# A message-passing layer: six edge chunks of unequal size, three packed lists, and eight quads whose rows are gathered from x and multiplied on the chip

## The chip, the core and the metric

The kernel runs on one core of a Trainium2 chip. The metric is the time of one execution on the device in microseconds; lower is better. The kernel before took 831.66 us (median of three runs, 831.54 to 835.16). A core has five engines, each of which runs its own instructions in program order: TensorE (PE in the profile, PEld its weight loads), VectorE (DVE), ScalarE (ACT), GpSimd (POOL) and SyncE (SP), which here only issues DMAs. Engines wait for each other through semaphores. SBUF is the memory on the chip, PSUM holds TensorE's sums, and DRAM tensors lie outside.

## What is computed

The input is a graph of 12,500 nodes with 128 features each (`x`) and 400,000 edges, sorted by their destination `dst`. Each edge has a source `src` and a length `d`.

```python
rbf = exp(-(d[:, None] - centers) ** 2 / (2.0 * width * width))      # 50 centers from 0 to 10
cut = 0.5 * (cos(pi * d / 10) + 1.0) * (d <= 10)
W = (silu(rbf @ fw1 + fb1) @ fw2 + fb2) * cut[:, None]
messages = (x[src] @ pw + pb) * W
agg = segment_sum(messages, dst)
y = x + (silu(agg @ mw1 + mb1) @ mw2 + mb2)
out = layernorm(x + y)
```

An edge longer than 10 counts for nothing, since `cut` is zero there. With these inputs 71,145 of the 400,000 edges remain.

## The kernel before, in words

**Order of the work.** The program order of every engine is written out by hand (`manual_schedule`). Python generators and loops decide it while the kernel is built; on the chip it is fixed, and an engine that waits holds all that stands behind in its order.

**Packing.** The edges come in five chunks of 128 rows of 625 edges. For each chunk `pack(c)`, a generator, drops the edges that are too long. VectorE counts how many are gone before each one (`gone`, `step`), joins step, destination and source in one word (`nodes`), and moves the words and the lengths to the left in ten passes by powers of two (lines 340 to 361). A row of at most 160 survivors (`CAP`, the tile `line`) is then written by one GpSimd scatter (line 382) to its place in the DRAM tensor `packed`. Rows overlap with zeros at their ends, so even rows go to one list and odd rows to another (`side`). The lists are cleared first. A read-back (`pair`, line 393) takes both lists and ORs them. The unpacking then gives source indices (`srci`), local destinations (`dl`), cutoff factors (`cut`) and bases, each turned by TensorE and copied to its place, and stores the lengths to DRAM (`near_d`). `yield` values are estimates of VectorE's time; the callers spend them as a budget (`advance`). Chunk 0 is read back by GpSimd, the others by SyncE.

**Projection.** Meanwhile all of `x` is loaded in 25 tiles of 512 nodes, turned (`turn`), multiplied by `pw` with the bias `pb` (`project`) and stored to the DRAM tensor `proj`. A bias is used as a sum of three bf16 parts, which VectorE makes (`in_parts`).

**The loop over quads.** A quad is 512 packed edges; there are 141. `fetch(q)` gathers the quad's rows of `proj` by four indirect DMAs from GpSimd (line 490) into one of eight buffers `got`. `radial`, `basis`, `first`, `tanh`, `silu` and `second` compute W for it. `message` multiplies (line 560), which frees the buffer. `place` makes one-hot matrices from `dl` and `cut` (line 568), `sum_up` multiplies with them, and `add` adds the sums into `aggT` (line 595), a 128 x 12,500 tile in SBUF that GpSimd has cleared. In each turn of the loop quad q + 3 is fetched (`AHEAD`), and VectorE goes on with packing the next chunks (`QB` tells which quads a chunk serves).

**Nodes.** From quad 70 on (`NODES`), whenever the sums of 512 nodes are final, the node network and the layer norm run between the quads; the rest follows after the last quad. Behind everything stands a branch that computes the whole again without packing; with these inputs it is not taken.

Of the kernel before, what the change touches and what calls it, by code (L numbers as in the profile page):

```python
# [29 lines left out]
RB = 8  # L30
CAP = 160


QB = (0, 26, 54, 81, 109, 141)
NC_ = len(QB) - 1
NQ = QB[-1]
AHEAD = 3
GOT = 8

# [6 lines left out]
def kernel(  # L46
# [40 lines left out]
    R = E // (NC_ * P)  # L87
# [3 lines left out]
    assert H == P and E == NC_ * P * R and E % P == 0 and W <= N <= 1 << SB  # L91
    assert CAP <= R < 1 << (32 - RB - SB) and 2 * MW % P == 0
# [32 lines left out]
    def load_rows(c):  # L125

        raw[c] = []
        for name, ap, dt in (("r_d", edge_weight, I32), ("r_dst", dst, I32), ("r_src", src, I32)):
            t = work.tile([P, R], dt, name=name, bufs=2)
            v = ap[c * P * R:(c + 1) * P * R].rearrange("(r l) -> r l", r=P)  # L130
            nc.sync.dma_start(t, v if ap is not edge_weight else v.bitcast(I32))
            raw[c].append(t)
# [9 lines left out]
    zero_i = keep.tile([P, 2 * MW // (4 * P)], I32, name="zero_i")  # L142
    nc.gpsimd.memset(zero_i, 0)
    packed = dram.tile([2, MW], I32, name="packed")
    for k in range(4):
        nc.gpsimd.dma_start(packed.rearrange("s (k w) -> (s k) w", k=P // 2)
                            .rearrange("p (q w) -> p q w", q=4)[:, k], zero_i)
    aggT = keep.tile([P, N], F32, name="aggT")

    def clear(a, b):  # L150

        for n0 in range(a, b, 500):
            nc.gpsimd.memset(aggT[:, n0:min(n0 + 500, b)], 0.0)

    clear(0, 3500)
# [18 lines left out]

    def load_weights():
        for p0 in (0, 64):
            nc.sync.dma_start(w1_sb[p0:p0 + NUM_RBF], fw1)
            nc.sync.dma_start(w1_sb[p0 + NUM_RBF:p0 + KR], row(fb1))
        return (load_bias("fb2", fb2), load_bias("mb1", mb1), load_bias("mb2", mb2),
                load("fw2_sb", [H, H], fw2), load("mw1_sb", [H, H], mw1),  # L180
                load("mw2_sb", [H, H], mw2))
# [12 lines left out]
    for name in ("pb", "fb2", "mb1", "mb2"):  # L194
# [9 lines left out]
    nc.vector.tensor_scalar(before, iota_n[:, :P], part_f, None, op0=OP.is_gt)  # L204

    side_i = keep.tile([P, 1], I32, name="side_i")
    nc.vector.tensor_scalar(side_i, part_i, 1, None, op0=OP.bitwise_and)
    side = keep.tile([P, 1], F32, name="side")
    nc.vector.tensor_scalar(side, side_i, float(MW), None, op0=OP.mult)

    end = keep.tile([P, 1], F32, name="end")
    nc.vector.tensor_scalar(end, part_f, 2.0, float(2 * NQ * QE), op0=OP.mult, op1=OP.add)

    k_f = keep.tile([P, 1], F32, name="k_f")
    nc.vector.tensor_scalar(k_f, part_f, 64.0, -64.0, op0=OP.is_ge, op1=OP.mult)
    nc.vector.tensor_add(k_f, k_f, part_f)
    rbf_scale = keep.tile([P, 1], F32, name="rbf_scale")
    nc.vector.tensor_scalar(rbf_scale, k_f, float(NUM_RBF), None, op0=OP.is_lt)  # L220
    rbf_bias = keep.tile([P, 1], F32, name="rbf_bias")
    nc.vector.tensor_scalar(rbf_bias, k_f, -CUTOFF / (NUM_RBF - 1), rbf_scale,
                            op0=OP.mult, op1=OP.mult)

    def in_parts(name, t):
        b = bias_b[name]
        p = keep.tile([96, H], BF16, name=name + "_p")
        for k in range(3):
            nc.vector.tensor_copy(p, t)
            nc.vector.tensor_copy(b[32 * k:32 * k + 1],  # L230
                                  p[32 * k:32 * k + 1, None, :].to_broadcast([1, 4, H]))
            if k < 2:
                nc.vector.tensor_sub(t, t, p)
        return b
# [22 lines left out]
    for c in range(NC_):  # L257
        nc.vector.tensor_scalar(lim[:, c:c + 1], part_f[:64], float(2 * QB[c] - DONE[1]), 0.0,
                                op0=OP.add, op1=OP.max)
    nc.vector.scalar_tensor_tensor(lim, lim, DONE[0], lim, op0=OP.mult, op1=OP.mult)  # L260
# [26 lines left out]
    bits = (R - 1).bit_length()  # L287
    LB = RB + SB

    def rowed(dt, name, n=R, bufs=1):  # L290
        return work.tile([P, n], dt, name=name, bufs=bufs)

    def pack(c):

        if c + 1 < NC_:
            load_rows(c + 1)
        r_d, r_dst, r_src = raw[c]
# [5 lines left out]
        yield 0.6  # L303
        gone = rowed(F32, "gone")
        nc.vector.tensor_tensor_scan(gone, drop, drop, 0.0, op0=OP.add, op1=OP.max)
        yield 1.4
# [4 lines left out]
        yield 0.9  # L311
# [10 lines left out]
        yield 0.6  # L322
        relc = rowed(F32, "drop")
        nc.vector.tensor_scalar(relc, rel, -127.5, None, op0=OP.add)
        yield 0.4
        nc.vector.tensor_reduce(span[:, c:c + 1], relc, AX.X, OP.max, apply_absolute_value=True)
        yield 0.7
# [4 lines left out]
        yield 0.3  # L332
# [3 lines left out]
        yield 0.7  # L336
        nc.vector.scalar_tensor_tensor(nodes, step, LB, nodes, op0=OP.logical_shift_left,
                                       op1=OP.bitwise_or)
        yield 0.7
        for b in range(bits):  # L340
# [6 lines left out]
            yield 0.4  # L347
            m = go[:, k:n + k]
            if b < bits - 1:
# [4 lines left out]
                yield 0.7  # L354
# [4 lines left out]
            yield 0.7  # L359
            nc.vector.copy_predicated(r_d[:, :n], m, r_d[:, k:n + k])  # L360
            yield 0.7
# [15 lines left out]
        line = work.tile([P, CAP, 2], I32, name="line", bufs=2)  # L377
# [3 lines left out]
        yield 0.6  # L381
        nc.gpsimd.indirect_dma_start(
            out=packed.rearrange("s (w o) -> (s w) o", o=1),
            out_offset=bass.IndirectOffsetOnAxis(ap=at_i[:, 0:1], axis=0),
            in_=line.rearrange("p e w -> p (e w)"), in_offset=None)
        if c == 0:
            clear(3500, N)
        yield -3
# [3 lines left out]
        pair = work.tile([64, 2, 512], I32, name="pair", bufs=1)  # L392
# [67 lines left out]

    xT_of = {}

    def turn(t0):
        r = rows(t0)
        n = sum(r)
        xp = bank("pu")
# [323 lines left out]
    for k, t0 in enumerate(tiles):  # L790
        if k + 6 < len(tiles):
            load_x(tiles[k + 6])
        if k == 4:
            weights = load_weights()
# [166 lines left out]
```

## Time and profile before

| what | value |
|---|---|
| median of the runs | 831.66 us |
| profiled execution | 830.76 us |
| its span, first to last instruction | 829.0 us |
| instructions | 11346 |
| TensorE, share of the span busy | 71% |
| VectorE | 82% |
| GpSimd | 70% |
| ScalarE | 31% |
| bytes moved by DMA | 90.62 MB |
| first gather of rows starts | 71.60 us |
| first message starts | 85.73 us |
| last gather starts | 801.92 us |

A line of a group reads: source line, engine, operation, tile written <- tiles read, how many, then busy time in us and the mean of one in ns, and after the second bar the idle time of the engine just before them and what ended it. "issue" is time in which an engine waited for nothing that the profile shows. A line of a timeline reads: start and length in us, then the instruction, and in brackets the engine's idle time before it and what ended that. The granted clock is TensorE's, as a share of full speed.

### The profile page before, as it was taken

How to read it: one execution, taken by the hardware profiler on the slowest of the kernel's cores; microseconds unless marked ns; L12 is line 12 of the kernel's file. 1: busy time of each engine (PE TensorE's matmuls, PEld its weight loads, DVE VectorE, ACT ScalarE, POOL GpSimd, SP SyncE). 2: the span in 40 equal slices, each digit the busy share in tenths (PEclk: the TensorE clock that was granted, in tenths of full speed). 3: DMA queues.
4: the chain of work that ended last, by engine and by line, in shares of the span. 5: the costliest groups of instructions: out<-in, count | busy, mean ns of one | idle time of the engine just before them, and what ended most of it. 6: DMA issues, size and time to landing. Idle time of an engine off the chain costs nothing.

```text
span 829.0 us, 11346 instructions
## 1 busy us (share of the span) xinstructions
PE 588.0 (71%) x3356; PEld 449.8 (54%) x3356; DVE 679.6 (82%) x1822; ACT 257.6 (31%) x397; POOL 578.6 (70%) x613
## 2 busy tenths in 40 slices
PE   4792766666667766776767687787877876867862
PEld 4680545455555555555555465555655664646651
DVE  7967899989999998999968888777867667667774
ACT  2454322132222322232222233523434424521521
POOL 3045777777777777777777777777777777777750
PEclk9995788878887788768896799998999988999887
DMA  8994324232153323233333442722623623632421
GB/s 245 265 309 122 96 64 128 72 103 76 49 151 77 90 73 80 58 97 88 88 83 92 102 118 77 195 66 78 181 77 89 169 80 87 171 99 52 122 61 41
DMA packets 85700, 90.62 MB, mean 109 GB/s; under 512 B 13623, under 2 KB 64851, under 8 KB 85632
## 3 DMA queue, kind: packets, MB, share of 16 engines
q1 hardware_dynamic: 66464, 49.95, 21.1%
q0 software_dynamic: 18912, 39.77, 19.4%
q8 instruction: 28, 0.46, 0.2%
q14 instruction: 40, 0.33, 0.1%
q10 hardware_dynamic: 256, 0.11, 0.1%
HBM read 74.71 MB, written 15.07 MB: 108 GB/s over the span
## 4 chain that ended last, share of the span: by engine, by line
DVE 33%; POOL 17%; PE 16%; DMA 15%; issue 14%; DVEq 3%; ACT 1%; SPq 1%; POOLq 0%; ACTq 0%
POOL got L490 16%; DMA got<-proj,srci 11%; DVE hot L568 8%; DVE s L542 4%; PE pa L577 4%; DVE msg L560 3%; DVE aggT L595 3%; PE ph L529 3%; PE pu L554 3%; DMA x<-in_x_dram 3%; DVEq L585 2%; DVE r_d L360 2%; PE pa L242 1%; PE ms L242 1%; DVE st L629 1%
## 5 line engine op out<-in xcount | busy, mean ns | idle before, releaser
L490 POOL DMA_INDIRECT got<-proj,srci x564 | 553.8, 982 | 171.9 <-issue 146.6
L577 PE MATMUL pa<-hot,msg 128*128 128x128 f32 x1128 | 184.6, 315 | 107.1 <-DVE msg L560 106.8
L577 PEld LDWEIGHTS pa<-hot,msg 128*128 128x128 f32 x1128 | 164.3, 224 | 121.4 <-DVE msg L560 121.3
L554 PEld LDWEIGHTS pu<-fw_h,s 128*128 128x128 f32 x1128 | 176.2, 223 | 12.0 <-issue 5.1
L554 PE MATMUL pu<-fw_h,s 128*128 128x128 f32 x1128 | 174.8, 306 | 0.0
L568 DVE TENSOR_SCALAR hot<-iota_n,dl,cut 128x128 f32<-128x128 f32 x564 | 158.0, 356 | 0.8 <-PE pa L577 0.6
L535 ACT ACTIVATE t<-ph 128x1024 f32<-128x1024 f32 (+1 forms) x71 | 71.8, 1012 | 268.5 <-PE ph L529 255.0
L529 PE MATMUL ph<-rbf,w_sb 51*128 51x512 f32 x282 | 101.3, 791 | 63.9 <-DVE s L542 53.3
L560 DVE TENSOR_TENSOR msg<-pu,got 128x512 f32<-128x512 f32 x141 | 96.3, 683 | 60.4 <-DMA got<-proj,srci 49.1
L542 DVE SCALAR_TENSOR_TENSOR s<-t,ph 128x1024 f32<-128x1024 f32 (+1 forms) x71 | 85.7, 1207 | 6.8 <-ACT t L535 6.7
L595 DVE TENSOR_TENSOR aggT<-aggT,pa 128x128 f32 x282 | 79.9, 283 | 7.5 <-PE ms L607 2.3
L529 PEld LDWEIGHTS ph<-rbf,w_sb 51*128 51x128 f32 x282 | 27.8, 224 | 85.3 <-issue 52.6
L551 PE MATMUL pu<-fb_b,ones_b 96*128 96x512 bf16 x141 | 61.7, 438 | 0.0
L609 ACT ACTIVATE zt<-ms 128x512 f32<-128x512 f32 (+1 forms) x25 | 14.6, 587 | 150.3 <-PE ms L607 150.3
L519 ACT ACTIVATE rbf<-d,rbf_bias,rbf_scale 128x512 f32<-128x512 f32 (+1 forms) x71 | 57.1, 804 | 0.2
L668 ACT ACTIVATE x<-x,by,rs 128x128 f32<-128x128 f32 x91 | 37.3, 482 | 59.4 <-DVE by L638 59.4
L551 PEld LDWEIGHTS <-ones_b 96*128 96x128 bf16 x141 | 14.9, 105 | 73.7 <-issue 73.2
L520 ACT ACTIVATE rbf<-rbf 128x512 f32<-128x512 f32 (+1 forms) x71 | 44.7, 630 | 2.2
L351 DVE SCALAR_TENSOR_TENSOR nodes<-go,nodes 128x625 int32<-128x625 int32 x45 | 36.5, 810 | 1.3
L360 DVE COPY_PREDICATED r_d<-go,r_d 128x624 int32<-128x624 int32 (+9 forms) x50 | 36.9, 739 | 0.0
L355 DVE COPY_PREDICATED nodes<-go,nodes 128x624 int32<-128x624 int32 (+8 forms) x45 | 35.9, 798 | 1.2
L626 DVE SCALAR_TENSOR_TENSOR x<-x,ms 128x512 f32<-128x512 f32 x23 | 15.8, 686 | 24.9 <-PE ms L242 24.9
(159 smaller groups left out, 501.1 us busy)
## 6 DMA issues: line engine op xcount, KB each, us to landing
d<-near_d SPq DMA_DIRECT2D x137, 128.0 KB
x<-in_x_dram SPq DMA_DIRECT2D x48, 256.0 KB
got<-proj,srci POOLq DMA_INDIRECT x564
proj<-hp SPq DMA_DIRECT2D x24, 256.0 KB
out_dram<-x SPq DMA_DIRECT2D x24, 256.0 KB
r_d<-in_edge_weight_dram SPq DMA_DIRECT2D x5, 312.5 KB
r_dst<-in_dst_dram SPq DMA_DIRECT2D x5, 312.5 KB
r_src<-in_src_dram SPq DMA_DIRECT2D x5, 312.5 KB
```

The lines of the kernel that those rows point to most:

```text
L360: nc.vector.copy_predicated(r_d[:, :n], m, r_d[:, k:n + k])
L490: nc.gpsimd.indirect_dma_start(out=got[:, j, :], out_offset=None, in_=proj, in_offset=bass.IndirectOffsetOnAxis(ap=i, axis=0))
L519: nc.scalar.activation(rbf[:u], d[:u], AF.Square, bias=rbf_bias[:u], scale=rbf_scale[:u])
L529: nc.tensor.matmul(ph[:, h, :], w1_sb[p0:p0 + KR], rbf[p0:p0 + KR], start=True, stop=True)
L535: nc.scalar.activation(t[:, :n], ph[:, :n], AF.Tanh, scale=0.5)
L542: nc.vector.scalar_tensor_tensor(s[:, :n], t_of.pop(o)[:, :n], 1.0, ph[:, :n], op0=OP.add, op1=OP.mult)
L551: nc.tensor.matmul(pu, ones_b[:, :P], bias_b["fb2"].rearrange("k j f -> k (j f)"), start=True, stop=False)
L554: nc.tensor.matmul(pu[:, j * H:(j + 1) * H], s[:, j * P:(j + 1) * P], fw2_h, start=False, stop=(j == QT - 1))
L560: nc.vector.tensor_mul(msg, pu_of.pop(q).rearrange("p (j f) -> p j f", j=QT), got_of.pop(q))
L568: nc.vector.tensor_scalar(hot[:, j, :], iota_n[:, :W], dl[:, at[0], at[1]], cut[:, at[0], at[1]], op0=OP.is_equal, op1=OP.mult)
L577: nc.tensor.matmul(pa[:, k * W:(k + 1) * W], msg[:, j, :], hot[:, j, :], start=(j % 2 == 0), stop=(j % 2 == 1))
L595: nc.vector.tensor_add(to, to, pa[:, k * W:(k + 1) * W])
```

## The change

- **Chunks.** Six chunks of 180, 435, 600, 640, 640 and 630 edges a row (`ROWS`, `CAPS`, `QB`). The number of passes follows from the width: eight, nine and ten.
- **Three lists.** A row goes to the list of its number modulo 3; the read-back takes three lists and needs one more OR. The lists are cleared in three stages (`clear_packed`), the first by GpSimd, the others by SyncE (at tile 12 and behind quad 1).
- **Rows of x.** The first eight quads (`FROM_X`) are gathered from `x` instead of `proj`, before the projection is finished, and turned and multiplied by `pw` in their buffers (`multiply`).
- **Clearing.** ScalarE clears `aggT` by copies scaled by zero (`clear`): ten pieces of 500 during the projection, the other fifteen from quad 32 on. Bases of chunks 0 to 2 stay below 5000.
- **Parts of a bias.** ScalarE makes the bf16 copies (`part_of`); VectorE keeps the subtraction.
- **Order by estimated times.** Estimates of VectorE's time now depend on the width (`one`, `two_a_cycle`). A clock of VectorE (`clock`), one of GpSimd (`pool`) and the times at which rows have landed (`there_at`) decide where a fetch, a packing step, a multiplication or a read-back is put into the orders (`fetches`, `multiplies`, `pack_until`). Fetches may now stand up to eight quads ahead (`GOT`) instead of three. The read-backs' lengths (`radials`) are copied by SyncE alone; two of these four pairs were GpSimd's in the kernel before.

```diff
-CAP = 160
-QB = (0, 26, 54, 81, 109, 141)
+ROWS = (180, 435, 600, 640, 640, 630)
+CAPS = (58, 128, 160, 166, 166, 164)
+QB = (0, 7, 26, 52, 80, 109, 141)
...
+FROM_X = 8
 GOT = 8
+CLEARED = 5000
+CLEAR_Q = 32
+CLEAR_C = 2
+PACK_US = (1.4, 1.0)
...
-    packed = dram.tile([2, MW], I32, name="packed")
-    for k in range(4):
-        nc.gpsimd.dma_start(packed.rearrange("s (k w) -> (s k) w", k=P // 2)
-                            .rearrange("p (q w) -> p q w", q=4)[:, k], zero_i)
+    packed = dram.tile([3, MW], I32, name="packed")
+    def clear_packed(k, eng):
+        a, b = CLEAR[k:k + 2]
+        for i in range(3):
+            v = packed[i, a:b].rearrange("(p w) -> p w", p=P)
+            for w0 in range(0, (b - a) // P, 376):
+                n = min(376, (b - a) // P - w0)
+                eng.dma_start(v[:, w0:w0 + n], zero_i[:, :n])
+    clear_packed(0, nc.gpsimd)
...
-        for n0 in range(a, b, 500):
-            nc.gpsimd.memset(aggT[:, n0:min(n0 + 500, b)], 0.0)
+    def clear(pieces=1, to=N):
+        while pieces and to_clear and to_clear[0][0] < to:
+            a, b = to_clear.pop(0)
+            nc.scalar.activation(aggT[:, a:b], iota_n[:, :b - a], AF.Copy, scale=0.0)
+            pieces -= 1
...
+    def part_of(name, t, k):
+        p = keep.tile([96, H], BF16, name=f"{name}_p{k}")
+        nc.scalar.copy(p, t)
+        nc.scalar.copy(bias_b[name][32 * k:32 * k + 1],
+                       p[32 * k:32 * k + 1, None, :].to_broadcast([1, 4, H]))
+        if k < 2:
+            nc.vector.tensor_sub(t, t, p)
...
+    def one(n):
+        return 0.1 + 0.00115 * n
+    def two_a_cycle(n):
+        return 0.1 + 0.0007 * n
...
+    def fetches(until, most):
+        while fetched[0] < min(most, known[0]) and pool[0] <= until:
+            q = fetched[0]
+            fetch(q, table=x if q < FROM_X else None)
+            pool[0] = max(pool[0], summed.get(q - GOT, 0.0)) + 5.15
+            there_at[q] = pool[0] + 2.2
+            fetched[0] += 1
...
+        fetches(clock[0], most[0])
+        pool[0] = max(pool[0], clock[0]) + 1.35
         nc.gpsimd.indirect_dma_start(
             out=packed.rearrange("s (w o) -> (s w) o", o=1),
...
+        awake[c] = pool[0] + (2.6 if c == 0 else 3.5)
...
+        nc.vector.tensor_tensor(pair[:np_, 0], pair[:np_, 0], pair[:np_, 1], OP.bitwise_or)
+        yield 0.6
+        nc.vector.tensor_tensor(length, pair[:np_, 0, 1::2], pair[:np_, 2, 1::2], OP.bitwise_or)
...
+    def multiply(q):
+        turn("got", got_of[q])
+        h = bank("pa").rearrange("p (k f) -> p k f", k=4)
+        rows_times(h, xT_of.pop("got"), pw_sb, bias_b["pb"], [P] * 4)
+        nc.scalar.copy(got_of[q], h)
...
+    def pack_until(us, ahead=2):
+        while clock[0] < us and todo:
+            c = next((c for c in todo[:ahead] if awake[c] <= clock[0]), None)
+            if c is None:
+                clock[0] = min([us] + [awake[c] for c in todo[:ahead]])
+            else:
+                go_on(c)
+    def multiplies(until):
+        while times[0] < min(FROM_X, fetched[0]) and there_at[times[0]] <= until:
+            multiply(times[0])
+            times[0] += 1
...
     for k, t0 in enumerate(tiles):
...
+        if loads and k >= 4:
+            nc.sync.dma_start(*loads.pop(0))
+        if k == 12:
+            clear_packed(1, nc.sync)
+        if k == 18:
+            load_rows(2)
+        if k in (19, 20, 21):
+            part_of("fb2", fb2_f, k - 19)
         project(t0)
+        clear(1, CLEARED)
...
+        upto = 12.0 + 2.1 * k
+        fetches(upto, FROM_X)
+        multiplies(upto)
+        pack_until(upto, 1 if 0 in todo and 1 not in todo else 2)
+        if k >= 16:
+            radials(3)
...
     for q in range(NQ):
         nodes(q)
-        if q + AHEAD < NQ:
-            fetch(q + AHEAD)
+        most[0] = min(NQ, q + GOT)
+        fetches(clock[0], most[0])
+        fetches(math.inf, min(NQ, q + AHEAD + 1))
+        multiplies(max(clock[0], there_at[min(q + 1, NQ - 1)]))
+        if q >= CLEAR_Q:
+            clear()
+        radials(q // 2 + 5)
...
-        left = 1.3 if q % 2 == 0 else 2.5
-        for c in list(todo[:2]):
-            if rest[c]:
-                rest[c] -= 1
-            elif left > 0:
-                left = advance(c, left)
+        clock[0] = max(clock[0], there_at[q])
+        summed[q] = clock[0] + 0.7
+        clock[0] += 2.2 if q % 2 else 3.4
+        if q == 1:
+            clear_packed(2, nc.sync)
+        if q + 1 < NQ:
+            pack_until(max(there_at[q + 1], clock[0] + PACK_US[min(todo, default=0) > CLEAR_C]))
```

## The prediction

> **What bounds the kernel now.** I read the page's busy shares first, then the chain, then GpSimd's own waits and its timeline, and last VectorE in two stretches. VectorE looks like the bound by share (82% against GpSimd's 70%), but shares hide idle time that an engine cannot avoid.
>
> From the page (part 1, the chain, the group of the gather):
>
> ```profile
> PE 588.0 (71%) x3356; PEld 449.8 (54%) x3356; DVE 679.6 (82%) x1822; ACT 257.6 (31%) x397; POOL 578.6 (70%) x613
> DVE 33%; POOL 17%; PE 16%; DMA 15%; issue 14%; DVEq 3%; ACT 1%; SPq 1%; POOLq 0%; ACTq 0%
> L490 POOL DMA_INDIRECT got<-proj,srci x564 | 553.8, 982 | 171.9 <-issue 146.6
> ```
>
> The 564 gathers (four for each of 141 quads) cost 982 ns each, and each has 171.9/564 = 0.305 us of idle time ahead of it, nearly all "issue": GpSimd waits for nobody. Its own list of waits (total, times, longest) says the same: no entry of a gather has a longest wait over 0.3 us, and the long ones lie ahead of the first gather.
>
> ```profile
> POOL got L490 <- issue: 146.6, 481, 0.3
> POOL packed L382 <- DVE first L300: 40.6, 1, 40.6
> POOL near_d L402 <- DVE length L401: 8.1, 1, 8.1
> POOL got L490 <- DMA got<-proj,srci: 7.9, 26, 0.3
> ```
>
> Its timeline gives the ends of that stretch (start, length, then the instruction):
>
> ```profile
> 48.95 1.06 POOL L382 DMA_INDIRECT packed<-line,at_i  x1 [40.59 <-DVE first L300]
> ...
> 71.60 1.18 POOL L490 DMA_INDIRECT got<-proj,srci  x1 [0.30 <-DVE part L277]
> ```
>
> and, further on, quad 8's first gather and the last gather of all:
>
> ```profile
> 113.33 1.31 POOL L490 DMA_INDIRECT got<-proj,srci  x1 [0.30 <-issue]
> ...
> 801.92 0.94 POOL L490 DMA_INDIRECT got<-proj,srci  x1 [0.30 <-issue]
> ```
>
> From 71.60 to 802.86 GpSimd goes from gather to gather: 564 x (0.982 + 0.305) = 725.9, plus four scatters of packed rows at about 1.35 with their gap, 731.3 in all. So the span is 71.6 before the first gather + 731.3 + 26.1 after the last (829.0 - 802.86). VectorE is a close second. In 85 to 425 us, while lists are packed between the quads, it is busy 318.87 of 340 us and its list of waits shows no wait for a gather from 100 to 400; afterwards it is busy 281.76 of 378.
>
> ```profile
> 85.00:425.00 340.00, 239.75 (x1273) 184.56 (x1271) 318.87 (x769) 85.17 (x107) 261.94 (x257) 0.80 0.32 86
> 425.00:803.00 378.00, 287.09 (x1679) 214.53 (x1680) 281.76 (x852) 130.24 (x216) 286.18 (x301) 0.90 0.41 107
> ```
>
> The columns are PE, PEld, DVE, ACT, POOL, clock, DMA share and GB/s.
>
> **The change, part by part.** What matters is when the gathers of quad 8 and later can run. Eight buffers hold gathered rows, so quad 8's gather waits until quad 0's message is made. From there on GpSimd has the same 133 quads to gather, 802.86 - 113.33 = 689.5 us, and the same 26.1 behind it. So I time quad 0's message.
>
> *Chunk 0 packed (180 edges a row in place of 625).* VectorE does this. A shifting pass of 625 took 3.0 us (four instructions: 0.50, 0.81, 0.86, 0.74 by the groups of L345, L351, L355, L360), and instructions of 113 to 160 columns took 0.23 to 0.33. Between these, a pass takes 1.15 at 180 columns and 2.3 at 435. The bias's casts move to ScalarE, where a 128x512 copy takes 0.59. The bias landed at 6.07 in before, so VectorE's first subtraction of it, which now stands ahead of the scan, holds the scan to about 6.6. Then come scan 0.5, the seven small side instructions 0.9 (0.13 each), counts, steps and the second subtraction 0.7, the offsets up to the first joined word 2.3, seven passes 7.6 (the last are narrower), the last pass 0.6 and seven line instructions 1.4: the scatter starts at 20.6, where it stood at 48.95. Scatter 1.1, landing 2.5 (the chain's landings of gathers are 2.3 to 2.8), read-back 0.7 to issue and 2.5 to land give 27.4. VectorE fills that wait with 1.7 us of small instructions, which had lain before the packing, and chunk 1's head. From the read-back to the indices took 66.36 to 68.56 = 2.2; the third list adds an OR of 512 words, about 0.65 (twice the 0.41 of 256 less the overhead). Indices at 30.3, **first gather at 30.5 instead of 71.6**. The four copies of lengths that GpSimd issued ahead of it (522 ns each) go to SyncE. The 25 clears of 532 ns leave GpSimd; only 18 of them (8.3 us) stood behind the first scatter, beside waiting for it, so they are inside the 41 us and not added again. On ScalarE 25 x 0.59 = 15 us lie in an engine that is busy 31%; ten are in the projection, the others at quads 32 to 46, each between two additions into the same sums. A clear finds its addition done a quad earlier, so I cost these at nothing; 15 x 0.6 = 9 us on VectorE if that cover is gone.
>
> *Gathers beside the packing.* Here one rule of the Trainium skill speaks against the change. The rows: from 100 to 400 us, beside packing, a gather took 1022 ns; from 500 to 800, with none, 947 ns.
>
> ```profile
> L490 POOL DMA_INDIRECT got<-proj,srci x224 | 228.9, 1022 | 68.3 <-issue 59.7 <-DMA got<-proj,srci 4.0 <-DVE aggT L595 2.4
> L490 POOL DMA_INDIRECT got<-proj,srci x240 | 227.2, 947 | 73.1 <-issue 59.7 <-DVE aggT L595 4.3 <-DMA got<-proj,srci 2.7
> ```
>
> The skill's page "SBUF — State Buffer", section "A bandwidth-pool intuition that's wrong (but worth ruling out)", says that GpSimd cannot write descriptors while VectorE holds the port they share: a GpSimd-issued DMA of some 620 ns alone took some 3100 beside a VectorE copy, five times as long. By that, the first 20 gathers beside chunk 1's packing would take 20 x (5 x 0.947 + 0.305) = 101 us and end at 131; with three more quads quad 8 would start near 148 instead of 113.3, and the kernel would be 35 us slower. By the row they take 20 x (1.022 + 0.305) = 26.5 and end at 57. I take the row: it is this gather beside these very instructions.
>
> *Chunk 1 (435 edges a row).* The rest of chunk 0's unpacking took 68.56 to 75.77 = 7.2, so 37.5. One joining instruction 0.6, eight passes 17.9, the last 1.0, lines 2.0 with the new subtraction: scatter at 59. It stands behind 20 gathers in GpSimd's order, and makes it wait 2 us; quads 5 and 6 follow to 71. VectorE does chunk 2's head and one pass, 8.7, to 67.7. The read-back is SyncE's, behind the projection's stores of tiles 18 to 22 (and ahead of the lengths for quad 6 on). TensorE, in whose order chunk 0's last transposes stand behind tile 9, waits for them until 37.6; one tile took it 1.55 us where nothing delayed it (39.5 to 50 us), and 13 tiles and 5 gathered quads are 28: tile 22 at 65.5, stored at 66.2, the read-back lands at 69.2. Unpacking 2.9 + 7.2 ends at 79.3. Quad 7, which needs chunk 1's indices, is gathered from 72.5 to 78.
>
> *To the first message.* From the last unpacking copy (ends 75.77) to the first message (85.73) took 10.0, in order ScalarE's basis, two first layers, one second layer. Two first-layer products took 2.08 there at a clock of 0.58; busier TensorE, 1 us less: 9.0. **First message at 88.3, quad 8's gather at 89**, against 113.3.
>
> *Multiplying eight quads.* Each adds to TensorE about a tile's 1.55 and to ScalarE two copies of 0.59. Six fall in the projection (counted). Two fall beside quads 0 to 2, where transposes take a PSUM bank between two second layers, so that one second layer waits for a message: some 3 us there, half of it hidden in VectorE's packing. I take 1.5; between 0 and 4.
>
> *VectorE after that.* I added VectorE's instructions between messages in both program orders, each at its row's duration, scaled by width: the changed one has 15% less per quad up to quad 40 than before had in its packing quads, and 1% less from 41 to 80. Before's packing quads ran at 5.35 us (quad 0's message at 85.73, quad 61's at 411.9), VectorE full. So 4.5 us up to quad 40, 5.3 to quad 80. GpSimd takes 4 x 1.327 = 5.3. VectorE, eight quads behind at 89, catches up near quad 40 and then goes level. The scatters of chunks 2 to 5 stand in GpSimd's order 3 to 8 quads behind the message after which their lines are ready: margins of 12, 13, 10 and 17 us. No wait. The packing left at quad 8 is some 12% more than before had at its quad 8: about 2 us more of slow gathers (of 17 = 224 x 0.075). The clearing of lists and the smaller first loads move bytes, some 17 MB before the loop in both, at 240 to 306 GB/s.
>
> **Sum.** 89.0 + 689.5 + 26.1 + 1.5 + 2.0 = 808.1 of span. The profiled execution took 830.76 for 829.0 of span, so 809.9; the median of the runs is 0.9 above it: **810.8 us**, 2.5% faster.
>
> **Rivals.** *(a) An earlier start.* The chain to the first message runs ten us shorter, as projection and unpacking fit: message at 78, 800 us. For it: the work itself up to 59 has no wait in it; against: the waits behind the stores.
> *(b) Half lost.* VectorE or the banks lose 5 to 17 us: 815 to 827.
> *(c) The start does not move.* The 2 MB gathered from x join a stage at 0.83 to 1.05 DMA share, products wait on them, stores and the read-back behind the stores come 20 us later: 828 to 836.
> *(d) Slower: GpSimd waits at its own scatters.* Its order is now fixed by estimates. If VectorE takes over 10 us longer than figured by quad 59, the scatter behind quad 62 holds the gathers, us for us; gain gone at 10 + 21 = 31 us, or 0.53 us (11%) per quad; at 0.8 us per quad the time is 848. For it: VectorE has no idle time in packing, and nodes' work (from quad 70) now overlaps packing. Against: the counts above.
>
> **How the numbers follow.** Likeliest case 0.45 (804 to 817 alone); (a) 0.20; (b) 0.17; (c) 0.06; (d) 0.12. A measurement tells 0.5% (827.5 to 835.8) from no change: faster 0.45 + 0.20 + 0.17 = 0.82, same 0.06, slower 0.12. The range, 796 to 828, leaves out (c), (d) and a little of (a).
>
> **What would show it.** First gather near 30 us, quads 0 to 4 at 1.3 us a gather, one wait of 2 us at chunk 1's scatter, gathers of quad 8 near 89, none of GpSimd's later waits over 2 us, last gather near 782. I am wrong if gathers beside chunk 1 take 2 us or more, if quad 8 starts after 100, or if GpSimd waits long at a scatter.

## The result, and the profile after

The changed kernel takes **837.96 us** (median of 13 runs, 836.51 to 842.32); the kernel before took 833.8 us beside it (13 runs, 830.03 to 836.07). The ratio is 1.0059, with an interval of 1.0041 to 1.0077: 0.6% slower, where 2.5% faster was forecast. The time lies above the range of 796 to 828. The profiled execution took 838.23 us for a span of 836.5, so the sum below is made against the span, 836.5 in place of the predicted 808.1. Three of the experiments below were first run while the kernel before itself took 1137 us; those first ratios (bias parts 0.988, no multiplication 0.973, loop after the indices 0.958) are left out, and a second run of each is used.

The page (busy shares, the chain, and the two groups of gathers):

```profile
PE 602.8 (72%) x3472; PEld 463.4 (55%) x3472; DVE 682.1 (82%) x1877; ACT 290.7 (35%) x463; POOL 568.6 (68%) x584
DVE 35%; PE 20%; DMA 13%; POOL 12%; issue 11%; ACT 3%; DVEq 3%; SPq 0%; POOLq 0%; ACTq 0%
L570 POOL DMA_INDIRECT got<-proj,srci x532 | 524.4, 986 | 183.7 <-issue 134.7
L570 POOL DMA_INDIRECT got<-in_x_dram,srci x32 | 33.5, 1048 | 25.4 <-DVE part L502 16.2
```

A gather costs what it cost (986 ns; 982 before), so the difference is in what GpSimd waits for. Its list of waits (total, times, longest) names it:

```profile
POOL got L570 <- issue: 142.9, 446, 7.3
...
POOL got L570 <- DVE part L502: 16.2, 2, 15.2
...
POOL got L570 <- ACT xT L544: 13.1, 1, 13.1
...
POOL pair L457 <- DMA packed<-line,at_i: 5.0, 1, 5.0
POOL packed L442 <- DVE line L438: 3.8, 1, 3.8
```

Before, the long waits all stood ahead of the first gather. Now three single waits of 15.2, 13.1 and 7.3 us stand among the gathers (the list writes "issue" for the third because nothing in the profile names its cause; an experiment below does). GpSimd's timeline gives their places (start, length, instruction):

```profile
20.02 1.03 POOL L442 DMA_INDIRECT packed<-line,at_i  x1 [15.60 <-DVE k_f L247]
26.05 0.63 POOL L457 DMA_DIRECT2D pair<-packed  x1 [5.00 <-DMA packed<-line,at_i]
...
33.54 1.02 POOL L570 DMA_INDIRECT got<-in_x_dram,srci  x1 [1.05 <-DVE part L502]
...
65.19 0.99 POOL L442 DMA_INDIRECT packed<-line,at_i  x1 [3.85 <-DVE line L438]
...
91.55 0.94 POOL L570 DMA_INDIRECT got<-in_x_dram,srci  x1 [15.19 <-DVE part L502]
...
109.35 0.94 POOL L570 DMA_INDIRECT got<-proj,srci  x1 [13.11 <-ACT xT L544]
...
544.37 0.94 POOL L570 DMA_INDIRECT got<-proj,srci  x1 [7.31 <-issue]
...
808.55 0.97 POOL L570 DMA_INDIRECT got<-proj,srci  x1 [0.30 <-DMA got<-proj,srci]
```

The first gather moved from 71.60 to 33.54, but quad 7's stands at 91.55, behind 15 us of waiting for chunk 1's indices, and quad 8's at 109.35, behind 13 us of waiting for quad 0's message (107.92 to 108.61) to free a buffer. The line names ScalarE's copy `xT`, which ended last (109.23), 0.6 us behind the message; without the multiplications, below, the same line names the message. Quad 8's gather was forecast for 89 and had stood at 113.33; "quad 8 starts after 100" was one of the prediction's own signs of being wrong. Of a start brought forward by 38 us, 4 are left eight quads later. From there:

| part of the span | before | forecast | after |
|---|---|---|---|
| to quad 8's first gather | 113.3 | 89.0 | 109.35 |
| quad 8 to the end of the last gather | 689.5 | 693.0 | 700.2 |
| behind the last gather | 26.1 | 26.1 | 27.0 |
| span | 829.0 | 808.1 | 836.5 |

Without the 7.3 us wait at 544 the second row is 692.9. The two windows that the prediction shows of the kernel before now read:

```profile
85.00:425.00 340.00, 237.84 (x1299) 183.12 (x1299) 298.16 (x740) 102.94 (x137) 245.12 (x242) 0.80 0.31 90
425.00:803.00 378.00, 291.68 (x1687) 216.03 (x1688) 304.32 (x875) 135.50 (x224) 282.00 (x293) 0.89 0.39 106
```

VectorE is busy 298 us of the first stretch (319 before) and 304 of the second (282): packing has moved later, as planned. A gather from 100 to 400 us took 1016 ns (1022 before), from 500 to 800 us 948 (947 before).

### The profile page after: what moved, and what is told of

Same layout as the page of the kernel before. It is cut to its first block, busy times and chain, and to the rows that moved or that the text cites. A ratio compares the mean times of both kernels' runs of the same rounds, so it can differ in the third digit from the quotient of the medians.

```text
span 836.5 us, 11685 instructions
## 1 busy us (share of the span) xinstructions
PE 602.8 (72%) x3472; PEld 463.4 (55%) x3472; DVE 682.1 (82%) x1877; ACT 290.7 (35%) x463; POOL 568.6 (68%) x584
## 4 chain that ended last, share of the span: by engine, by line
DVE 35%; PE 20%; DMA 13%; POOL 12%; issue 11%; ACT 3%; DVEq 3%; SPq 0%; POOLq 0%; ACTq 0%
POOL got L570 12%; DMA got<-proj,srci 10%; DVE hot L654 8%; DVE s L628 5%; PE pa L663 4%; PE ph L615 4%; DVE msg L646 4%; PE pu L640 3%; DVE aggT L681 3%; DVEq L671 2%; PE pa L267 2%; PE ms L693 2%; DVE r_d L418 2%; DMA pair<-packed 1%; PE ms L267 1%
## 5 line engine op out<-in xcount | busy, mean ns | idle before, releaser
L570 POOL DMA_INDIRECT got<-proj,srci x532 | 524.4, 986 | 183.7 <-issue 134.7
L663 PE MATMUL pa<-hot,msg 128*128 128x128 f32 x1128 | 181.6, 312 | 103.0 <-DVE msg L646 102.7
L663 PEld LDWEIGHTS pa<-hot,msg 128*128 128x128 f32 x1128 | 162.3, 222 | 115.4 <-DVE msg L646 115.2
L640 PE MATMUL pu<-fw_h,s 128*128 128x128 f32 x1128 | 172.9, 304 | 0.0
L570 POOL DMA_INDIRECT got<-in_x_dram,srci x32 | 33.5, 1048 | 25.4 <-DVE part L502 16.2
L267 PEld LDWEIGHTS pa<-pw_sb,xT 128*128 128x128 f32 (+1 forms) x260 | 38.4, 216 | 14.4 <-ACT xT L544 13.2
L267 PE MATMUL pa<-pw_sb,xT 128*128 128x128 f32 (+1 forms) x260 | 40.2, 304 | 8.1 <-ACT xT L544 8.1
L409 DVE SCALAR_TENSOR_TENSOR nodes<-go,nodes 128x640 int32<-128x640 int32 (+4 forms) x51 | 36.5, 716 | 1.6
```

Of the source, the lines that this page charges most:

```text
L267: nc.tensor.matmul(to[:m, k, :], lT[:, k * P:k * P + m], w, start=False, stop=(k == a + c - 1))
L570: nc.gpsimd.indirect_dma_start(out=got[:, j, :], out_offset=None, in_=proj if table is None else table, in_offset=bass.IndirectOffsetOnAxi ...
L640: nc.tensor.matmul(pu[:, j * H:(j + 1) * H], s[:, j * P:(j + 1) * P], fw2_h, start=False, stop=(j == QT - 1))
L663: nc.tensor.matmul(pa[:, k * W:(k + 1) * W], msg[:, j, :], hot[:, j, :], start=(j % 2 == 0), stop=(j % 2 == 1))
```

## The experiments

**Theory A**: the start of quad 8 is held by a row of waits, each passed on in some engine's program order: the rows of chunk 2 come late, VectorE waits for them, TensorE's tiles wait in turn, the stores come late, and chunk 1's read-back stands behind the stores on SyncE; the 7.3 us at 544 are the load of the count into a register (VectorE makes the number `bad_i`, which every engine reads for the branch behind everything). **Rival B**: the stage is bound by the bytes it moves, and another order moves nothing. A third possibility is that gathers and multiplications of x cost more than they bring.

What the traces show (us; edits below). The ratio is to the kernel before, timed beside each. The places in us are those of one profiled execution, so a difference of 1 us between two rows is not more than two executions of like kernels can show: "count late" differs from the changed kernel only from quad 84 on, and its read-back is issued 1.1 us earlier.

| kernel | chunk 1's read-back issued / used | first message | quad 8's gather | last gather ends | ratio and interval |
|---|---|---|---|---|---|
| changed kernel | 80.7 / 88.4 | 107.9 | 109.4 | 809.5 | 1.0059 (1.0041 to 1.0077) |
| rows early | 78.4 / 86.1 | 105.6 | 107.0 | 807.3 | 1.0009 (0.9986 to 1.0031) |
| bias parts early | 83.1 / 90.8 | 110.3 | 111.7 | 812.1 | 1.0075 (1.0054 to 1.0096) |
| no multiplication | 75.9 / 83.6 | 102.7 | 103.7 | 803.1 | 1.0018 (1.0001 to 1.0036) |
| count late | 79.6 / 86.8 | 106.3 | 107.7 | 804.3 | 0.9989 (0.9971 to 1.0006) |
| no rows of x | 74.4 / 81.8 | 101.1 | 129.2 | 819.3 | 1.0187 (1.0148 to 1.0226) |
| four moves | 77.1 / 85.0 | 104.5 | 105.9 | 801.1 | 0.9939 (0.9918 to 0.9960) |
| + read-back by GpSimd | 73.0 / 81.6 | 101.1 | 102.6 | 797.8 | 0.9902 (0.9868 to 0.9935) |
| four moves + early loop | 76.3 / 84.5 | 92.3 | 100.6 | 794.0 | 0.9879 (0.9850 to 0.9908) |
| both | 69.0 / 78.4 | 94.1 | 102.9 | 799.9 | 0.9901 (0.9864 to 0.9937) |
| both, five quads of x | 70.3 / 81.3 | 92.5 | 100.7 | 796.4 | 0.9888 (0.9853 to 0.9924) |
| read-back by GpSimd, loop after the indices | 69.8 / 79.0 | 90.1 | 91.6 | 789.6 | 0.9872 (0.9845 to 0.9899) |

**Rows early.**

```diff
-        if k == 18:
+        if k == 10:
             load_rows(2)
```

> The rows of chunk 2 are loaded eight tiles earlier; nothing else is changed. Theory A (the start of quad 8 is set by waits that pass from engine to engine in program order): the 5.0 us wait of VectorE for r_dst goes, with it the waits behind it (ScalarE's cast 2.8, TensorE for xT 4.2, VectorE for the prefix 4.6); the read-back of chunk 1 is issued near 73 instead of 80.7, the first message comes at 99 instead of 107.9, and the kernel takes 829 in place of 838 (0.989 of the changed kernel). Rival B (the stage is bound by the bytes it moves): the same bytes only come in another order, the first message stays within 2 us of 107.9, and the kernel takes 836 to 840.

VectorE's wait for `r_dst` went, but the read-back came only 2.3 us earlier and quad 8 2.3 us. A wait took its place: VectorE stood 4.1 us for ScalarE's cast of the second bias, because ScalarE's copies of the tiles stood ahead of it, and chunk 1's scatter came at 67.9 instead of 65.2. The kernel is 0.5% faster than the changed one (1.0009 against 1.0059), some 4 us of the nine expected. Neither theory as it stood.

**Bias parts early.**

```diff
-        if k in (19, 20, 21):
-            part_of("fb2", fb2_f, k - 19)
+        if k in (13, 14, 15):
+            part_of("fb2", fb2_f, k - 13)
```

> The changed kernel with the three parts of the second bias made six tiles earlier. Theory (the late rows of chunk 2 reach TensorE through these parts): TensorE's 4.2 us wait for xT and VectorE's 4.6 us for the prefix go, the read-back of chunk 1 is issued 3 to 6 us ahead of 80.7; quad 8's gather at 103 to 106 in place of 109.4; 832 to 835 us. Rival (TensorE is late for another reason): the read-back within 1 us of 80.7, 837 to 839 us.

Theory A's link fell: no gain, and the read-back 2.3 us later. ScalarE's timeline shows why. The last two numbers are the length of the idle time and what ended it:

```profile
71.17 0.59 ACT L544 COPY xT<-pu 128x512 f32<-128x512 f32 x1
75.37 0.58 ACT L553 COPY hp<-pa 128x512 f32<-128x512 f32 x1 [3.60 <-DMA proj<-hp]
75.85 1.08 ACT L544 COPY xT<-pu 128x512 f32<-128x512 f32 x2
```

With the cast out of the way, ScalarE waits as long for a buffer whose store (`proj<-hp`) has not landed, and TensorE still waits 3.8 us for `xT` behind it (4.2 before). Between those stores stand the six loads of chunks 2 and 3 (67.4 to 73.6 us in SyncE's order). Read so, the loads can hold TensorE through the stores as well as through VectorE. In the changed kernel ScalarE's waits for these stores are 0.7 us in all, so there the second path, if it was open, lay hidden behind the first. That the stores are late because of the loads is read from SyncE's order; no run moves chunk 3's loads alone.

**No multiplication** (quads 0 to 7 use the rows of x themselves, so a part of the product is left out).

```diff
     def multiply(q):
-        turn("got", got_of[q])
-        h = bank("pa").rearrange("p (k f) -> p k f", k=4)
-        rows_times(h, xT_of.pop("got"), pw_sb, bias_b["pb"], [P] * 4)
-        nc.scalar.copy(got_of[q], h)
+        return
```

> The changed kernel without the multiplication of the eight gathered quads of x: their messages use the rows of x themselves, so that part of the product is left out; all loads, gathers and stores stay. Theory (TensorE's order with multiplications of 2.4 us each): the read-back of chunk 1 is issued near 71 in place of 80.7, quad 8's gather at 95 to 98 in place of 109.4; 823 to 827 us. Rival (bytes): quad 8's gather stays within 3 us of 109.4.

The read-back came at 75.9, quad 8 at 103.7, 5.7 us earlier: between the two expectations; 835.64 us. VectorE and TensorE of this kernel:

```profile
69.28 0.15 DVE L358 CAST first<-r_dst 128x1 f32<-128x1 int32 x1 [6.27 <-DMA r_dst<-in_dst_dram]
```

```profile
71.56 0.59 PE L372 MATMUL ms<-cnt,before 128*128 128x1 f32 x2 [5.74 <-DVE cnt L365]
```

TensorE reached chunk 2's prefix (`ms<-cnt,before`, a running count over the rows) earlier and then stood 5.7 us for VectorE, which stood 6.3 us for chunk 2's rows: they arrive at 69.3, hardly before the 69.9 of the changed kernel. SyncE asked for them at 62.8, not much ahead of 64.4, because ScalarE now waited 9.6 us for stores to land. The DMA engines were busy throughout: the share was 0.99 from 40 to 60 us and 1.02 from 60 to 70, where 1 means all sixteen engines busy and the profile's sum can pass it a little. So half of Theory A holds (the multiplications delay the stores), and there is something in Rival B: once the multiplications are gone, the stage runs into the transfers.

**Count late.**

```diff
-        elif counted and total is None:
+        elif counted and total is None and q > counted[0] + 7:
             total = nc.values_load(bad_i[0:1, 0:1], min_val=0, max_val=2 * E)
```

> GpSimd loads the count of edges into its register seven quads later in its order; nothing else is changed. Theory: the 7.3 us wait ahead of quad 88's gather goes, and the kernel gets 5 to 7 us shorter (831 to 833 in place of 838). Rival: GpSimd is some 20 us ahead of the messages at that place, so the wait only takes lead away that the end doesn't need, the same time is lost at buffers of gathered rows later, and the kernel stays at 836 to 839.

No wait of an issue is longer than 0.3 us now, and the ratio falls from 1.0059 to 0.9989, 5.8 us of 834. The register load caused the 7.3 us wait. Its rival (lead given up for nothing) falls as a whole, but not every us of the wait was worth one: in the profiled execution the stretch from quad 8's first gather to the end of the last takes 696.6 us in place of 700.2.

**No rows of x.**

```diff
-FROM_X = 8
+FROM_X = 0
```

> No quad gathers rows of x: all quads wait for the stored projection, and the multiplications of gathered rows go; the rest of the change stays. Theory: GpSimd cannot gather before the projection is stored, near 81 us, quad 0 to 4 come after that, quad 8's gather at 115 to 120 in place of 109.4, the kernel takes 843 to 850. Rival (the eight gathers of 2 MB and their eight multiplications cost the stage more than they bring): quad 8's gather at 109 or sooner, 838 or less.

```profile
POOL got L570 <- DMA proj<-hp: 22.7, 1, 22.7
```

GpSimd waits 22.7 us for the stored projection, its first gather is at 86.4, quad 8's at 129.2 and the kernel takes 850.81. So the gathers of x bring more than they cost. Quad 8 came later than expected: here the first message (101.1) is early, and GpSimd's own eight quads (42.8 us) are what is late. The kernel tells one thing more. With neither gathers nor multiplications of x, the read-back is issued at 74.4, 6.3 us ahead of the changed kernel; without the multiplications alone it was 4.8. The remaining 1.5 us, not far above the scatter of single executions, are what the 2 MB of gathers can have cost on this path.

**Four moves**: rows early, bias parts early, count late, and the rows of chunk 3 later:

```diff
-        if 1 < c < NC_ - 1:
+        if 2 < c < NC_ - 1:
             load_rows(c + 1)
...
         if q == 1:
             clear_packed(2, nc.sync)
+            load_rows(3)
```

> Four moves together: the rows of chunk 2 loaded eight tiles earlier, the bias's parts made six tiles earlier, the rows of chunk 3 loaded when quad 1 is reached instead of ahead of chunk 2's packing, the count's register load seven quads later. Theory A (waits in program order): the read-back of chunk 1 is issued near 70 and lands in 4 instead of 7.7 us, the first message comes near 95, quad 8's gather near 96 and no wait at quad 88; the kernel takes 814 to 822, less than the kernel before. Rival B (bytes): quad 8's gather not before 106, and only the 7 us of the count are gained: 829 to 834.

829.25 us (ratio 0.9939), faster than the kernel before and the changed one, but by the ratios 10 us below the changed kernel and not 16 to 24. TensorE goes through the tiles from 56 to 80 us with no wait over 0.6 us (one of 3.2, behind a store, is left at 52), so TensorE's coupled waits are gone; the read-back is issued at 77.05, still behind the last stores. It was expected to land in 4 us, without chunk 3's rows ahead of it. It took 7.9 (7.7 in the changed kernel): that cause of the landing falls.

**The read-back by GpSimd, and the loop.** First the four moves with

```diff
-        dma = nc.gpsimd if c == 0 else nc.sync
+        dma = nc.gpsimd if c <= 1 else nc.sync
```

> As the kernel with the four moves, but chunk 1's read-back is issued by GpSimd, behind quad 5's gathers, and no longer by SyncE behind the stores of the projection (there it was issued at 77.05 us and VectorE got it at 84.98). Theory A1 (the read-back is late because it stands behind the stores in SyncE's order and in their queue): it is issued near 71 and is there before 77; then TensorE is what is left, because the transposes of chunk 1's indices stand behind the last tile and quad 5's multiplication, which end near 80. Indices near 81 in place of 87.9, first message near 98, quad 8's gather near 99 in place of 105.9; 822 to 825 us in place of 829. Rival (read-backs of such a shape take 8 us beside the projection's transfers, whichever queue they are in, or the bytes are the bound): it is there at 79 or later, and the kernel stays at 827 to 830.

It was issued at 73.0, 4 us earlier, and was used at 81.6 without a wait for it. Quad 8 followed with 3.3 us. The reason given for the read-back being late (its place in SyncE's order) holds for 4 us; as to its duration the rival is nearer, since it takes about as long from GpSimd (last section). Then the four moves with

```diff
-    while todo[0] < 2:
+    while todo[0] < 1:
         pack_until(clock[0] + 1.0)
```

> As the kernel with the four moves, but the loop over the quads starts when chunk 0's lists are there, and chunk 1's unpacking is put between the first quads (its read-back stays with SyncE). Theory: the ten us from chunk 1's last copy to the first message no longer stand behind all of the unpacking; the first message comes at 93 to 97 in place of 104.5, but the indices of chunk 1 then come later (near 96), quad 7's gather behind them, and quad 8's gather at 100 to 103 in place of 105.9: 823 to 827 us in place of 829. Rival (the indices of chunk 1 decide, not the message): quad 8's gather at 108 or later, 831 or more.

The first message comes 12 us earlier (92.3, a little sooner than expected), quad 8's gather 5 us (100.6), and the kernel takes 824.27 us, both as expected. GpSimd now waits 19.2 us for chunk 1's indices, which stand behind that message. With both edits, and then with five quads of x:

> Both: chunk 1's read-back by GpSimd, and the loop starts when chunk 0's lists are there. Theory: the read-back is there near 77, so VectorE reaches the first message near 90 and chunk 1's indices near 91; quad 8's gather at 96 to 98, 9 us ahead of the kernel with the four moves: 819 to 822 us. If only one of the two binds, the time is that of the better of the two alone.

> As the last, with five quads of x rows in place of eight: quads 5 to 7 wait for the stored projection. Theory: a multiplication costs TensorE 2.4 us (transpose, ScalarE's copy, product, one behind the other), and three fall away, one ahead of the last stores and two beside the first quads; but quads 5 to 7 are gathered only from 83 on, 16 us, so quad 8's gather comes at 99 to 101: 1 to 4 us slower than the last. Rival (the multiplications are what the stage lacks): faster than the last by 2 us or more.

Both together bring nothing more (102.9; 827.65 us). In that kernel, chunk 1's indices come behind the first message (97.4) although its lists are there at 78.4, so the order of these two on VectorE decides. Five quads of x are no slower than eight (825.70 us, the intervals overlap): three gathers less from x, three multiplications less.

Last, the read-back by GpSimd with the loop put where that finding says, behind the indices and ahead of the rest of the unpacking:

```diff
-    while todo[0] < 2:
+    while known[0] < QB[2]:
         pack_until(clock[0] + 1.0)
```

> The kernel with the four moves and the read-back by GpSimd, whose loop starts when chunk 1's indices are made; the rest of chunk 1's unpacking is put between the first quads. Theory: the first message at 91 to 95 in place of 101.1, quad 8's gather at 92 to 96 in place of 102.6; 817 to 821 us. If the end does not follow the start of quad 8 us for us: 822 to 827.

GpSimd's timeline of this kernel:

```profile
69.78 1.22 POOL L457 DMA_DIRECT2D pair<-packed  x1
...
82.03 0.99 POOL L570 DMA_INDIRECT got<-in_x_dram,srci  x1 [1.02 <-DVE part L502]
...
91.56 0.94 POOL L570 DMA_INDIRECT got<-proj,srci  x1 [4.79 <-issue]
...
98.29 1.11 POOL L570 DMA_INDIRECT got<-proj,srci  x1 [1.90 <-ACT xT L544]
...
106.48 0.95 POOL L570 DMA_INDIRECT got<-proj,srci  x1 [3.28 <-issue]
```

Quad 7 is gathered at 82.0 and quad 8 at 91.6, 18 us ahead of the changed kernel and 2.6 from the forecast of 89. The median, 823.41 us (818.3 to 827.28), is 1.3% below the kernel before and the lowest ratio of all, though its interval overlaps that of the early loop. It is the second case of the expectation, 822 to 827: the end does not follow the start of quad 8 us for us. Against the same kernel with the loop in its old place, quad 8 starts 11 us earlier and the ratio falls by 0.3%, within the intervals. (The profiled execution, span 816.2, was the fastest of six.) Three waits of 1.4 to 3.3 us at quads 9 to 11 give back 5.7 us: the rest of chunk 1's unpacking now stands between messages 0, 1 and 2. Apart from the two with fewer quads of x, all these kernels move the same rows, tiles and lists, and with the same bytes quad 8 starts anywhere from 92 to 112. Bytes alone are not the bound.

## Why the prediction was wrong

**The step that failed** is in "Chunk 1", the time at which chunk 1's lists are back: "tile 22 at 65.5, stored at 66.2, the read-back lands at 69.2". The read-back was issued at 80.7 and used at 88.4, and everything behind it, first message and quad 8's gather, moved with it. That quad 8's gather hangs on the first message was right; what was wrong is the path to that message, which was priced without the waits between engines. SyncE's order shows where the read-back stood, behind the last stores:

```profile
70.90 9.64 SPq L133 DMA_DIRECT2D proj<-hp  x3
80.73 0.27 SPq L457 DMA_DIRECT2D pair<-packed  x1
```

VectorE, on the way from the late rows to the read-back, in the changed kernel:

```profile
69.88 0.15 DVE L358 CAST first<-r_dst 128x1 f32<-128x1 int32 x1 [4.97 <-DMA r_dst<-in_dst_dram]
...
77.41 0.16 DVE L375 TENSOR_TENSOR run<-run,cnt 128x1 f32<-128x1 f32 x1 [4.62 <-PE ms L374]
...
88.41 0.68 DVE L466 TENSOR_TENSOR pair<-pair 38x512 int32<-38x512 int32 x1 [5.05 <-DMA pair<-packed]
```

and TensorE in that stretch, one gathered quad that goes well and the one that waits:

```profile
44.37 0.60 PE L542 MATMUL pu<-ident,got 128*128 128x128 f32 x4
44.80 0.38 PE L264 MATMUL pa<-pb_b,ones_b 96*128 96x512 bf16 x1
45.79 1.16 PE L267 MATMUL pa<-pw_sb,xT 128*128 128x128 f32 x8 [0.61 <-ACT xT L544]
...
74.66 2.07 PE L267 MATMUL pa<-pw_sb,xT 128*128 128x128 f32 x8 [4.22 <-ACT xT L544]
```

Term by term, to quad 8's gather:

| term | forecast | measured | excess |
|---|---|---|---|
| TensorE waits for chunk 0's last transposes until | 37.6 | 41.0 | 3.4 |
| from there to the read-back's issue | 28.6 | 39.7 | 11.1 |
| read-back to VectorE | 3.0 | 7.7 | 4.7 |
| unpacking, to the last copy | 10.1 | 9.7 | -0.4 |
| to the first message | 9.0 | 9.85 | 0.85 |
| to quad 8's gather | 0.7 | 1.4 | 0.7 |
| sum | 89.0 | 109.35 | 20.35 |

- The 3.4 us: a gather's landing was taken for chunk 0's scatter and read-back. GpSimd waited 5.0 us for the scatter to land, and the read-back took 4.4. Indices and first gather came 3.0 us late (33.54 for 30.5). The DMA share from 21 to 30.5 us was 1.04, so the stretch was full of other transfers; the gathers' landings that were used as the measure came from the loop, where the share is 0.3 to 0.4, and even there some took up to 4.2 us.
- The 11.1 us: "each adds to TensorE about a tile's 1.55" was mis-sized. Two tiles overlap because `turn` runs ahead of the products; a gathered quad has transposes, ScalarE's copy and products one behind the other (44.37 to 46.79): 2.4 us, and 2.7 in the slow one beside its wait. Five are 12.5 in place of 7.75, so 4.7. The wait of 4.2 for `xT` was not in the working at all: chunk 2's rows, asked for at tile 18 (64.38 us), were not there when VectorE wanted them at 64.9. "One tile took it 1.55 us where nothing delayed it" was applied where something did. Behind that wait TensorE's granted clock was 0.50 (74.6 to 79.6 us; 1.00 from 55 to 70), and tile 22 took 2.4 us, about 1 more; 0.7 are the prefix products. Leaving the multiplications out brought 4.8 us of it, the four moves 3.7; the two overlap.
- The 4.7 us: "the read-back lands" in 3 us had no row. Before, chunk 0's was issued at 58.23 and used at 66.36 without a wait, so that trace bounded it by 8.1 us; that bound should have stood in the range. What made it 7.7 is in the last section: the transfer kept about two of the sixteen DMA engines busy.
- The last two, 0.85 and 0.7: "busier TensorE, 1 us less" did not come (the two first layers took 2.08 us each, as before), and quad 8's gather waited 0.6 us longer for ScalarE's copy than for the message.

**"689.5"** held in the changed kernel but for one omission. The count's register load stands in GpSimd's order behind quad 87's gather, which ends at 537.1, and VectorE makes the count after message 83:

```profile
542.89 0.14 DVE L849 CAST bad_i<-miss 1x1 int32<-1x1 f32 x1
```

Before, VectorE made the count at 461.6 and GpSimd read it at 461.7 with no wait. Now GpSimd's order runs further ahead: at quad 84 VectorE trails by 23.5 us, and the load takes 7.3 us of that lead. "Catches up near quad 40 and then goes level" was right to quad 40 and wrong behind it. Of the excess over 693.0 the count is nearly all; the gathers came 1.8 us slower in all for the 2.0 allowed, and a wait of 2.1 us at quad 9 stands for the 1.5 of the PSUM bank. But 689.5 is no constant: in the one kernel that starts quad 8 near the forecast (91.6), the stretch took 698.0 us, and its median is still 12.6 us above the forecast.

**What was right.** Chunk 0's scatter (20.02 for 20.6). Gathers beside packing at the row's price: the 32 gathers of x took 1048 ns (the first 20, beside the packing, 1100, and none over 1.37 us). By the rule that the prediction cites from the Trainium skill's page "SBUF — State Buffer", section "A bandwidth-pool intuition that's wrong (but worth ruling out)", taken for all of the packing, those 20 would have taken five times 947; no run here shows that. VectorE's pace to quad 40 (4.4 us a quad for 4.5, and 1.6 us behind GpSimd there). No wait at the scatters of chunks 2 to 5 (178.9, 306.4, 404.3 and 500.8), so rival (d) was wrong in its place though right in its sign. No wait of VectorE for ScalarE's clears shows in the trace.

**Which rival was right.** (c), "the start does not move": stores and the read-back behind the stores came 14.5 us late, on the path it named. Its reason, bytes, holds in part only. The DMA engines were full while VectorE and ScalarE waited for rows and stores (share 1.01 from 55 to 70 us, 1.05 from 70 to 74.6), so there is something in it; but the order of the work moved the start by 18 us with the bytes unchanged. It was given 6 in 100. Its range, 828 to 836, lacked the count: with that out of the way the kernel takes 833.62.

**What stays open.** How much of the stage's wait comes through VectorE and how much through the landing of stores cannot be told apart by the two edits, since either wait covers the other. Moving chunk 3's rows alone was not tried, nor more than eight buffers, which would loosen the tie between quad 0's message and quad 8's gather, nor a chunk 1 whose lists lie in another number of partitions.

## What to carry to other kernels

When a stage is brought forward, follow the resource that frees its successor (here the buffer, so the first message) through every queue that it passes: in this kernel each transfer ordered just in time for the old schedule became the next wait, and removing one uncovered another of nearly the same size. Price a load of a register by the lead of the engine that waits for it over the engine that writes it; a change that gives the first more lead makes the same instruction dear. Cost a detour by its dependent chain if nothing is pipelined around it, not by the busy time of its instructions.

## What the hardware did that was not expected

The time of a read-back of the packed lists does not follow its size, and the queue hardly matters. Chunk 1's (38 partitions, 228 KB) took 7.1 to 8.1 us from issue to use from SyncE in eight kernels, with or without 960 KB of row loads just ahead, and 9.2 us from GpSimd (1.2 of it the issue) in the one kernel where VectorE waited for it. Yet larger ones were quicker. In the changed kernel, all issued by SyncE:

| chunk | partitions, KB | issue to use, us | SyncE's queue while it moved: share of 16 DMA engines |
|---|---|---|---|
| 1 | 38, 228 | 7.7, waited for | 13.1% (85.0 to 88.1 us) |
| 2 | 52, 312 | 4.0 at most (181.46 to 185.42, no wait) | not read, other loads beside it |
| 4 | 58, 348 | 11.6, waited for (406.92 to 418.51) | 11.3% (407.9 to 417.8 us) |
| 5 | 64, 384 | not waited for | 72.2% (504.8 to 506.9 us, nearly all of its bytes) |

13.1% and 11.3% of sixteen engines are about two engines, 72.2% are about twelve. So the two slow read-backs were carried by about two engines at a time: SyncE's queue moved some 50 GB/s in chunk 1's stretch, where the whole stage from 40 to 60 us moved 274. They were not slow for full engines: in chunk 4's stretch the share of all queues together was 0.27. What sets the number of engines is not shown. The number of partitions differs between these rows, but so does all else that was running, and no run changes it alone.

Chunk 0's scatter landed late: GpSimd waited 3.9 to 6.0 us for it in the twelve kernels (5.0 in the changed one), where gathers on the chain of the kernel before landed in 2.3 to 2.8 for the most part, and in 4.2 at the longest. This does not show that a scatter is slower than a gather, since the DMA share was 1.04 there.
